# A graph layer with gathered rows: TensorE's waits for its own signals at reused PSUM slots

## The chip, the cores and the metric

The kernel runs on one core of one Trainium2 chip. The metric is the device time of that core in microseconds. The kernel before takes 18844.27 us, the median of three runs (18839.44 to 18869.69 us). One further execution was taken with the hardware profiler; it has its own, different time, given below.

## The reference

The layer works on a graph of 50,000 nodes with 160 features each and 1,650,000 directed edges, which come sorted by their destination. For each edge the features of the source node are multiplied with the four numbers of the edge (one scalar, one 3-vector) and with five small weight matrices; the messages are summed by destination node, multiplied with two more matrices, passed through a relu, added to the node's features twice, and normalised:

```python
s = x[:, :64];  v = x[:, 64:].reshape(n, 32, 3)
ss, vv = s[src], v[src]                      # gather by edge
e0, e1 = sh[:, 0:1], sh[:, 1:4]
out0 = C0 * (ss*e0 @ W1 + dot(vv, e1)*INV3 @ W2)
out1 = C1 * (p3(ss, W3, e1) + p4(vv*e0, W4) + p5(cross(vv, e1), W5))
m_agg = segment_sum(concat(out0, out1), dst)
h = concat(m_agg[:, :64] @ Ws * LIN_S, einsum(m_agg[:, 64:], Wv) * LIN_V)
x = layernorm(x + (x + relu(h)))
```

Everything after the gather is linear in the gathered row up to the relu, so a row of x can be summed per destination and per edge number first, and multiplied by combined weights afterwards.

## The kernel before, in words

**Tiling.** An edge slot is one of 128 partitions; 128 edges are a unit, six units a group, two groups a pair. There are 1,044 pairs. For each unit one indirect DMA on GpSimd's queue (POOL, L319 in `gather`) fetches 128 rows of x, one for each partition, into a sixth of a group's half of a tile `xg`; 12,522 such gathers make the whole edge list. The pool of `xg` holds four tiles, so four pairs can be in flight.

**Sums.** For each pair VectorE builds a selection matrix `ha` (L328, L331), 32 destinations by four edge numbers for each unit, and TensorE multiplies it with the gathered rows (L343 in `group_sums`), six matmuls adding up in each half of a PSUM tile `ps`. VectorE then turns the result into `sums` (L349). The pool `psA` has two slots for `ps`.

**Weights and nodes.** Four groups are a chunk of 128 sums. `apply_weights` multiplies a chunk by the weights (L579, five matmuls into the PSUM tile `phc`), and ScalarE copies it out. For each block of 128 nodes `own` makes the share of the node's own edge: two transposes of x into the PSUM tile `ptx` (L622), a copy by ScalarE to `xT` (L624), and twice two matmuls into a PSUM tile `yx` (L630), read by VectorE (L634, L636). `block` gathers the chunks that touch the block (L646, PSUM tile `phb`), adds, and starts the normalisation. The tiles `phc`, `ptx`, `yx` and `phb` share one tag, `misc`, in the pool `psM`, which has two slots.

**Order.** The program is written pair by pair; a table `later` (function `after_pair`) names what is to be issued after which pair: for a block, `do_ahead` (load x), four pairs later `do_own`, then `do_weights`, `do_block` and so on. A tile framework then draws the dependences between instructions and between a tile and the tile that had its slot before, orders each engine's instructions, and puts semaphore waits where a dependence needs one. An engine counts its finished work on a semaphore of its own; the one of TensorE is also waited for by TensorE itself, where it writes into a slot that it has written before: in the pair loop 1,280 of TensorE's matmuls carry such a wait (412 at L579, 337 at L646, 295 at L630, 234 at L343, 2 at L622).

Besides, the edge list is packed in the background: VectorE and SyncE rewrite the edges without the nodes' own edge into DRAM (`pack`), whose rows are loaded for later pairs.

Of the kernel before, what the change touches and what calls it, by code (L numbers as in the profile page):

```python
# [51 lines left out]
D = MUL0 + 3 * MUL1  # L52
# [10 lines left out]
W = 32  # L63
QG = P // W
FB = P // NK
ND = D // FB
# [38 lines left out]
def tile_gnn_resnorm(ctx: ExitStack, tc: tile.TileContext, x, src, dst, attr, W1, W2, W3, W4, W5, Ws, Wv, out, n_edges):  # L105
    nc = tc.nc
    N = x.shape[0]
    NBLK, NB, GA, G, NU, NG, L, NH, NR, FAR = plan(N, n_edges)
# [7 lines left out]
    ident = const.tile([P, P], F32, name="ident")  # L116
# [6 lines left out]
    BWh = const.tile([D // 2, 2, NK, D], F32, name="BWh")  # L123

    BWk = const.tile([P, ND, D], F32, name="BWk")
# [99 lines left out]
    with tc.tile_pool(name="once", bufs=1) as once, tc.tile_pool(name="raw", bufs=2) as rawp, \  # L225
# [98 lines left out]
        def spread(placed, u, n):  # L324
# [8 lines left out]
                                    .to_broadcast([P, n, NK, W]), op=ALU.mult)  # L333
            return ha

        def group_sums(p, rows, ha, at, i):


            s, g0, ng = pairs[p]
            ps = psA.tile([P, PG, D], F32, name="ps")  # L340
            rows, got = rows
            for j, xr in enumerate(rows):
                mm = nc.tensor.matmul(ps[:, j // G, :], ha[:, j].rearrange("p k w -> p (k w)"), xr,  # L343
                                      start=j % G == 0, stop=j % G == G - 1)

                if j == 0 and p + 1 < len(pairs):
                    for r in got[1:]:
                        tc.add_manual_dep(mm.ins, r.name, LANDED)
            nc.vector.transpose(at[:, :, i:i + ng, :].rearrange("p b g w -> p g b w"),  # L349
                                ps[:, :ng].rearrange("p g (b f) -> p g b f", f=FB))  # L350
# [224 lines left out]
        def apply_weights(at, ng):  # L575

            ph = psM.tile([P, D], F32, name="phc", tag="misc")
            for b in range(ND):
                nc.tensor.matmul(ph[:ng * W], at[:, b, :ng].rearrange("p g w -> p (g w)"), BWk[:, b, :], start=b == 0, stop=b == ND - 1)  # L579
            hp = hpp.tile([P, D], F32, name="hp")  # L580
            evict(hp[:ng * W], ph[:ng * W])  # L581
            return hp, ng * W

        def rows_of(b):
            nb = min(P, N - b * P)
            return nb, slice(b * P, b * P + nb)
# [6 lines left out]
        def ahead(bs):  # L593

            nb = rows_of(bs[0])[0]
            n0, n1 = rows_of(bs[0])[1].start, rows_of(bs[-1])[1].stop
            xt = aheadp.tile([P, BP, D], F32, name="xt")
            dq.dma_start(xt[:nb, :len(bs)], x[n0:n1, :].rearrange("(h n) d -> n h d", h=len(bs)))

            assert rows_stored[0] == NR or row_start(rows_stored[0])[1][0] >= n1  # L600
            sa = aheadp.tile([P, BP, NK], F32, name="sa")
            dq.dma_start(sa[:nb, :len(bs)],
                         selves[0, n0 * NK:n1 * NK].rearrange("(h n k) -> n h k", h=len(bs), k=NK))
            return [(xt[:, h], sa[:, h]) for h in range(len(bs))]
# [8 lines left out]
                                    rr[:, :len(cs)].unsqueeze(2).to_broadcast([P, len(cs), P]), op=ALU.is_equal)  # L613
            return hot2

        def own(b, xt, sa):

            nb, row = rows_of(b)
            H = D // 2
            pt = psM.tile([H, 2, P], F32, name="ptx", tag="misc")  # L620
            for i in range(2):
                nc.tensor.transpose(pt[:, i, :nb], xt[:nb, i * H:(i + 1) * H], ident[:nb, :nb])  # L622
            xT = np_.tile([H, 2, P], F32, name="xT")
            evict(xT[:, :, :nb], pt[:, :, :nb])  # L624
            t = aheadp.tile([P, D], F32, name="t")
            for h in range(NK // 2):
                y = psM.tile([P, 2, D], F32, name="yx", tag="misc")
                ks = slice(2 * h, 2 * h + 2)
                for i in range(2):
                    nc.tensor.matmul(y[:nb], xT[:, i, :nb], BWh[:, i, ks, :], start=i == 0, stop=i == 1)  # L630
                for i in range(2):
                    k = 2 * h + i
                    if k == 0:
                        nc.vector.tensor_scalar(t[:nb], y[:nb, i], sa[:nb, 0:1], None, op0=ALU.mult)  # L634
                    else:
                        nc.vector.scalar_tensor_tensor(t[:nb], y[:nb, i], sa[:nb, k:k + 1], t[:nb],  # L636
                                                       op0=ALU.mult, op1=ALU.add)
            return xt, t

        def block(b, xt, t, hot2):  # L640
            nb, row = rows_of(b)
            cs = of_block[b]
            ph = psM.tile([P, D], F32, name="phb", tag="misc")
            for i, c in enumerate(cs):
                hp, r = hps[c]
                nc.tensor.matmul(ph[:nb], hot2[:r, i, :nb], hp[:r], start=i == 0, stop=i == len(cs) - 1)  # L646
            nc.vector.tensor_tensor(ph[:nb], ph[:nb], t[:nb], op=ALU.add)  # L647
            return norm1(np_, ph[:nb], xt[:nb], nb)

# [5 lines left out]
        for h, (eng, period) in enumerate(HELP.items()):  # L655
            first = PG * G + h * period // 2
            nbatch = P // ROWS[eng]
            while True:
                at = [int(first + i * period / nbatch) // (PG * G) for i in range(nbatch)]
# [3 lines left out]
                s, g, ng = pairs[q]  # L663
# [47 lines left out]


        later = {}

        def after_pair(p, f, *args):
            later.setdefault(p, []).append((f, args))

        hps, of_nodes, resid, rstds, outs = {}, {}, {}, {}, {}
# [6 lines left out]
        def do_ahead(b):  # L725
            bs = together(b)
            if b == bs[0]:
                of_nodes.update(zip(bs, ahead(bs)))

        def do_own(b):  # L730
            of_nodes[b] = own(b, *of_nodes.pop(b))
# [30 lines left out]
        def examine_all():  # L762

            far = chunk_
            parts = [(c0, c1, near(c0 + 1) - near(c0), *bounds[c0]) for c0, c1 in zip(cuts, cuts[1:])]
            for c0, c1, each, low, high in parts:
                nc.vector.tensor_scalar(far[:, c0:c1], far[:, c0:c1], -each, c0 * each - near(c0) - (low + high) / 2,
                                        op0=ALU.mult, op1=ALU.add)
            nc.vector.tensor_tensor(far, far, rowid, op=ALU.add)
            for c0, c1, each, low, high in parts:  # L770
                nc.vector.tensor_scalar(far[:, c0:c1], far[:, c0:c1], 2 / (high - low), None, op0=ALU.mult)
            checks = ((extremes[:, 0], ALU.min, 0.0, ALU.is_lt), (extremes[:, 1], ALU.max, W - 1.0, ALU.is_gt),
                      (packed[:, 0], ALU.min, 0.0, ALU.is_lt), (packed[:, 1], ALU.max, 0.0, ALU.is_gt),
                      (counts[:, 0], ALU.min, 0.0, ALU.is_lt), (counts[:, 0], ALU.max, 0.0, ALU.is_gt),
                      (counts[:, 1], ALU.min, W / 2, ALU.is_lt),
                      (strayed, ALU.min, 0.0, ALU.is_lt), (strayed, ALU.max, 0.0, ALU.is_gt),
                      (far, ALU.min, -1.0, ALU.is_lt), (far, ALU.max, 1.0, ALU.is_gt))
            worst = once.tile([P, len(checks)], F32, name="worst")
            wrong = once.tile([P, len(checks)], F32, name="wrong")
            for i, (what, op, limit, cmp) in enumerate(checks):  # L780
                nc.vector.tensor_reduce(worst[:, i:i + 1], what, axis=AX.X, op=op)
                nc.vector.tensor_scalar(wrong[:, i:i + 1], worst[:, i:i + 1], float(limit), None, op0=cmp)
            bad = once.tile([P, 1], F32, name="bad")
            nc.vector.tensor_reduce(bad, wrong, axis=AX.X, op=ALU.max)
            pb = psM.tile([1, 1], F32, name="pb", tag="misc")
            nc.tensor.matmul(pb, bad, ones[:, 0:1], start=True, stop=True)
            nc.vector.tensor_scalar(more[:, 0:1], pb, 1.0, None, op0=ALU.min)
            nc.vector.tensor_scalar(more[:, 1:2], pb, 1.0, float(NB), op0=ALU.min, op1=ALU.mult)
# [4 lines left out]
        START = 2  # L793
        AHEAD = 7
        raws, has, flags = {}, {}, []
# [14 lines left out]
        for at, bs in zip(complete, after):  # L810
            for b in bs:
                after_pair(max(at - AHEAD, START - 1), do_ahead, b)
                after_pair(max(at - AHEAD + 4, START), do_own, b)
        later_pools.enter_context(tc.manual_schedule(engines={ET.SP}))
        for p, (s, g, ng) in enumerate(pairs):
# [68 lines left out]
    with tc.tile_pool(name="up", bufs=1) as up, tc.tile_pool(name="us", bufs=2) as us, tc.For_i(0, once_more, 1):  # L884
        nc.gpsimd.iota(base, pattern=[[NBLK, NB]], base=0, channel_multiplier=0, allow_small_or_imprecise_dtypes=True)
        dall = up.tile([P, JU, P], I32, name="dall")
        mm = up.tile([P, 2, JU], F32, name="mm")
# [14 lines left out]
        for s in range(nseg):  # L902
# [7 lines left out]
            for c in range(CB):  # L910
# [3 lines left out]
                at = us.tile([PB, 2, SEG], F32, name="at")  # L914
# [18 lines left out]
    with tc.tile_pool(name="edges2", bufs=2) as ep, tc.tile_pool(name="ops2", bufs=2) as op, \  # L933
            tc.tile_pool(name="node2", bufs=1) as np_, tc.tile_pool(name="psA2", bufs=2, space=PSUM) as psA, \
            tc.tile_pool(name="psF2", bufs=1, space=PSUM) as psF:
        with tc.For_i(0, blocks, 1) as b:
# [5 lines left out]
            with tc.For_i(u0, u1, GA) as u:  # L942
# [21 lines left out]
                ps = psA.tile([NBLK, 2, 512], F32, name="ps2")  # L964
                for j in range(GA):
                    for h in range(2):
                        nc.tensor.matmul(ps[:, h, 0:2 * D], hot[:, j, :], xa[:, j, 2 * h:2 * h + 2, :],
                                         start=j == 0, stop=j == GA - 1)
# [3 lines left out]
            for h in range(2):  # L972
                pt = psF.tile([D // 2, NK, P], F32, name="pt2")
                for k in range(NK):
                    nc.tensor.transpose(pt[:, k, :NBLK], acc[:, k, h * (D // 2):(h + 1) * (D // 2)], ident[:NBLK, :NBLK])
                at = np_.tile([D // 2, NK, NBLK], F32, name=f"ac{h}")
                nc.scalar.copy(at, pt[:, :, :NBLK])
                parts.append(at)
            ph = psF.tile([NBLK, D], F32, name="ph2")
# [45 lines left out]
```

## Time and profile before

| what | value |
|---|---|
| median of three runs | 18844.27 us |
| the profiled execution, its own time | 15704.38 us |
| span of its trace, first to last instruction | 15702.1 us |
| granted clock of TensorE | 0.724 |
| gathers on POOL, L319 | 12,522, 947 ns each |
| POOL busy | 11859.1 us (76%) |
| TensorE busy | 8274.5 us (53%) |
| VectorE busy | 6000.0 us (38%) |
| ScalarE busy | 498.2 us (3%) |
| DMA | mean 77 GB/s, q0 (the gathers) 24.6% of 16 engines' span |

The profiled execution is shorter than the runs without a profile by a factor of 15704.38 / 18844.27 = 0.833. Durations below are those of the profiled execution. A row of the profile names the line, the engine, what is written and read, how often, the total and mean time of one, and then how long the engine had been idle just before these instructions and what ended that idle time; "issue" is idle time that no signal in the trace explains.

### The profile page before, as it was taken

Reading aid. Unit: us, or ns where it says so; the run is one execution under the profiler, and the core shown is the slowest. Engines: PE = TensorE matmul, PEld = TensorE weight load, DVE = VectorE, ACT = ScalarE, POOL = GpSimd, SP = SyncE. Lnnn points to the kernel's source line nnn. Section 1 sums busy time; section 2 is a strip of 40 time slices with the busy share of each in tenths; the row PEclk is TensorE's granted clock in tenths of the full one; section 3 lists DMA queues with packets and bytes.
Section 4 is the critical chain, followed back from the end, with each engine's and each line's share of the span. In section 5 each row is a group of like instructions: output and inputs, shape, how many; then the busy total and the mean of one; then the engine's idle time right before and its main releaser. Section 6 shows DMA issues by size and latency. Waiting matters only on the chain. (4 is left out here: it accounts for less than half of the span.)

```text
span 15702.1 us, 120546 instructions
## 1 busy us (share of the span) xinstructions
PE 8274.5 (53%) x38505; PEld 7583.2 (48%) x38506; DVE 6000.0 (38%) x11070; ACT 498.2 (3%) x1392; POOL 11859.1 (76%) x12536
## 2 busy tenths in 40 slices
PE   4554555545555555555555555555555555555455
PEld 4444445445454444444444444444444445444454
DVE  5343433424334343443433434243343433434332
ACT  0000000000000000000000000000000000000000
POOL 7777777777777777777777777777777777777777
PEclk7777777777777776777777777777777767777677
DMA  2322222232322222222232232322223232222222
GB/s 79 86 73 84 74 77 80 72 86 73 85 73 77 81 73 78 80 76 81 73 86 72 77 82 72 86 72 78 79 74 85 72 86 73 75 80 73 75 74 67
DMA packets 797530, 1215.80 MB, mean 77 GB/s; under 512 B 271491, under 2 KB 575800, under 8 KB 792918
## 3 DMA queue, kind: packets, MB, share of 16 engines
q0 software_dynamic: 601056, 1026.60, 24.6%
q1 hardware_dynamic: 194410, 180.15, 3.9%
q8 instruction: 323, 5.29, 0.1%
q14 instruction: 301, 2.47, 0.1%
q10 hardware_dynamic: 1440, 1.29, 0.0%
HBM read 1135.77 MB, written 71.40 MB: 77 GB/s over the span
## 5 line engine op out<-in xcount | busy, mean ns | idle before, releaser
L319 POOL DMA_INDIRECT xg<-in_x,si x12522 | 11854.8, 947 | 3824.4 <-issue 3784.1
L343 PE MATMUL ps<-xg,ha 128*128 128x160 f32 x25044 | 5770.9, 411 | 7141.4 <-DMA xg<-in_x,si 5348.5
L343 PEld LDWEIGHTS ps<-xg,ha 128*128 128x128 f32 x25044 | 5512.6, 283 | 7455.4 <-issue 6701.9
L349 DVE STREAM_TRANSPOSE sums<-ps 128x320 f32<-128x320 f32 x1044 | 536.6, 515 | 7498.8 <-PE ps L343 7472.8
L331 DVE TENSOR_TENSOR ha<-hot,pk 128x1536 f32<-128x1536 f32 x1044 | 1805.9, 1731 | 64.4 <-PE ps L343 64.4
L630 PE MATMUL yx<-BWh,xT 80*128 80x320 f32 x3128 | 1099.9, 498 | 125.3 <-ACT xT L624 123.0
L579 PE MATMUL phc<-BWk,sums 128*128 128x160 f32 x5220 | 852.6, 312 | 11.6 <-DVE t L636 10.2
L630 PEld LDWEIGHTS yx<-BWh,xT 80*128 80x128 f32 x3128 | 642.1, 216 | 423.7 <-ACT xT L624 195.4
L579 PEld LDWEIGHTS phc<-BWk,sums 128*128 128x128 f32 x5220 | 788.7, 201 | 23.8 <-issue 20.1
L634 DVE TENSOR_SCALAR t<-yx,sa 128x160 f32<-128x160 f32 x391 | 147.0, 376 | 1414.3 <-PE yx L630 1412.2
L328 DVE TENSOR_TENSOR hot<-bank,rel 128x384 f32<-128x384 f32 x1044 | 557.5, 540 | 0.1
L646 PE MATMUL phb<-hp,hot 128*128 128x160 f32 x3474 | 550.7, 303 | 0.8 <-ACT hp L581 0.8
L646 PEld LDWEIGHTS phb<-hp,hot 128*128 128x128 f32 x3474 | 499.7, 192 | 24.7 <-issue 23.1
L636 DVE SCALAR_TENSOR_TENSOR t<-yx,sa,t 128x160 f32<-128x160 f32 x1173 | 438.4, 374 | 67.6 <-PE yx L630 59.7
L511 DVE COPY_PREDICATED prow<-marks,prow 128x2370 f32<-128x2370 int32 (+8 forms) x160 | 443.0, 2769 | 0.0
L581 ACT COPY hp<-phc 128x160 f32<-128x160 f32 x522 | 151.0, 289 | 7862.4 <-PE phc L579 7819.6
L624 ACT COPY xT<-ptx 80x256 f32<-80x256 f32 x391 | 143.5, 367 | 5866.1 <-PE ptx L622 5839.6
L511 DVE COPY_PREDICATED pra<-marks,pra 128x1580 f32<-128x1580 int32 (+8 forms) x160 | 303.6, 1898 | 0.0
L612 DVE TENSOR_TENSOR hot<-bank,rr 128x512 f32<-128x512 f32 (+2 forms) x391 | 285.1, 729 | 0.0
L647 DVE TENSOR_TENSOR phb<-phb,t 128x160 f32<-128x160 f32 x391 | 126.6, 324 | 109.1 <-PE phb L646 107.7
L622 PE MATMUL ptx<-ident,xt 128*80 128x128 f32 (+1 forms) x782 | 155.6, 279 | 20.6 <-ACT hp L581 18.4
L194 ACT ACTIVATE rstd<-mv,eps_t 128x1 f32<-128x1 f32 x391 | 115.2, 295 | 1334.1 <-DVE mv L189 1329.6
(144 smaller groups left out, 2612.5 us busy)
## 6 DMA issues: line engine op xcount, KB each, us to landing
xg<-in_x,si POOLq DMA_INDIRECT x12522
edges<-prow SPq DMA_DIRECT2D x1994, 18.5 KB
r<-edges SPq DMA_DIRECT2D x99, 360.0 KB
selves<-mine SPq DMA_DIRECT2D x1992, 0.5 KB
xt<-in_x SPq DMA_DIRECT2D x195, 160.0 KB
out<-o SPq DMA_DIRECT2D x195, 160.0 KB
pra<-in_attr SPq DMA_DIRECT2D x15, 1580.0 KB
pri<-in_src SPq DMA_DIRECT2D x15, 395.0 KB
```

The costliest lines, as they stand in the source:

```text
L319: got.append(nc.gpsimd.indirect_dma_start(out=xg[:, j, :], out_offset=None, in_=x, in_offset=bass.IndirectOffsetOnAxis(ap=placed[0][:, u + ...
L328: nc.vector.tensor_tensor(hot[:, :n], slotsP[:, 0:W].unsqueeze(1).to_broadcast([P, n, W]), rel[:, u:u + n].unsqueeze(2).to_broadcast([P, n ...
L331: nc.vector.tensor_tensor(ha[:, :n], hot[:, :n].unsqueeze(2).to_broadcast([P, n, NK, W]), pk[:, :, u:u + n].rearrange("p k u -> p u k").un ...
L343: mm = nc.tensor.matmul(ps[:, j // G, :], ha[:, j].rearrange("p k w -> p (k w)"), xr, start=j % G == 0, stop=j % G == G - 1)
L349: nc.vector.transpose(at[:, :, i:i + ng, :].rearrange("p b g w -> p g b w"), ps[:, :ng].rearrange("p g (b f) -> p g b f", f=FB))
L511: nc.vector.copy_predicated(what[:n, a:e], mi[:, r].unsqueeze(2).to_broadcast([n, e - a, what.shape[2]]), what[:n, a + d:e + d])
L579: nc.tensor.matmul(ph[:ng * W], at[:, b, :ng].rearrange("p g w -> p (g w)"), BWk[:, b, :], start=b == 0, stop=b == ND - 1)
L612: nc.vector.tensor_tensor(hot2[:, :len(cs)], slotsP.unsqueeze(1).to_broadcast([P, len(cs), P]), rr[:, :len(cs)].unsqueeze(2).to_broadcast( ...
L622: nc.tensor.transpose(pt[:, i, :nb], xt[:nb, i * H:(i + 1) * H], ident[:nb, :nb])
L630: nc.tensor.matmul(y[:nb], xT[:, i, :nb], BWh[:, i, ks, :], start=i == 0, stop=i == 1)
L636: nc.vector.scalar_tensor_tensor(t[:nb], y[:nb, i], sa[:nb, k:k + 1], t[:nb], op0=ALU.mult, op1=ALU.add)
L646: nc.tensor.matmul(ph[:nb], hot2[:r, i, :nb], hp[:r], start=i == 0, stop=i == len(cs) - 1)
```

## The change

A list `written` records, for each of the two kinds of PSUM slot (`ps` and `misc`), the matmuls that have written each tile. `wrote` declares to the framework, for a matmul that writes a tile, that it has no dependence on the matmuls of the tile allocated two before, which is the one that had the same slot. It is called for the first matmul of each half of `ps`, and for every matmul of `phc`, `ptx`, `yx` and `phb`. Nothing is declared about the readers on VectorE and ScalarE.

Besides, `own` is cut in two: `turned` has the two transposes and the copy to `xT`, `own` the four matmuls and what follows. `do_turned` is entered in the table just ahead of `do_own`, after the same pair.

```diff
+        written = {"misc": [], "ps": []}
+        def fresh(kind):
+            written[kind].append([])
+        def wrote(kind, ins):
+            ws = written[kind]
+            for old in ws[-3] if len(ws) > 2 else []:
+                tc.declare_no_dep(ins.ins, old, reason="its reader has waited for it")
+            ws[-1].append(ins.ins)
+            return ins
...
             ps = psA.tile([P, PG, D], F32, name="ps")
+            fresh("ps")
...
+                if j % G == 0:
+                    wrote("ps", mm)
+                else:
+                    written["ps"][-1].append(mm.ins)
...
             ph = psM.tile([P, D], F32, name="phc", tag="misc")
+            fresh("misc")
             for b in range(ND):
-                nc.tensor.matmul(ph[:ng * W], ...)
+                wrote("misc", nc.tensor.matmul(ph[:ng * W], ...))
...
-        def own(b, xt, sa):
+        def turned(b, xt, sa):
             pt = psM.tile([H, 2, P], F32, name="ptx", tag="misc")
+            fresh("misc")
             for i in range(2):
-                nc.tensor.transpose(pt[:, i, :nb], ...)
+                wrote("misc", nc.tensor.transpose(pt[:, i, :nb], ...))
             xT = np_.tile([H, 2, P], F32, name="xT")
             evict(xT[:, :, :nb], pt[:, :, :nb])
+            return xt, sa, xT
+        def own(b, xt, sa, xT):
...
+        def do_turned(b):
+            of_nodes[b] = turned(b, *of_nodes.pop(b))
...
+                after_pair(max(at - AHEAD + 4, START), do_turned, b)
                 after_pair(max(at - AHEAD + 4, START), do_own, b)
```

The matmuls of `yx` and `phb` are wrapped in the same way as those of `phc`.

More of the change, by code (lines that the diff above doesn't have):

```diff
@@ L577, in apply_weights @@
             ph = psM.tile([P, D], F32, name="phc", tag="misc")
+            fresh("misc")
             for b in range(ND):
-                nc.tensor.matmul(ph[:ng * W], at[:, b, :ng].rearrange("p g w -> p (g w)"), BWk[:, b, :], start=b == 0, stop=b == ND - 1)
+                wrote("misc", nc.tensor.matmul(ph[:ng * W], at[:, b, :ng].rearrange("p g w -> p (g w)"), BWk[:, b, :],
+                                               start=b == 0, stop=b == ND - 1))
             hp = hpp.tile([P, D], F32, name="hp")
@@ L614, in nodes @@
             return hot2
-        def own(b, xt, sa):
+        H = D // 2
+        def turned(b, xt, sa):
             nb, row = rows_of(b)
-            H = D // 2
             pt = psM.tile([H, 2, P], F32, name="ptx", tag="misc")
+            fresh("misc")
             for i in range(2):
-                nc.tensor.transpose(pt[:, i, :nb], xt[:nb, i * H:(i + 1) * H], ident[:nb, :nb])
+                wrote("misc", nc.tensor.transpose(pt[:, i, :nb], xt[:nb, i * H:(i + 1) * H], ident[:nb, :nb]))
             xT = np_.tile([H, 2, P], F32, name="xT")
             evict(xT[:, :, :nb], pt[:, :, :nb])
+            return xt, sa, xT
+        def own(b, xt, sa, xT):
+            nb, row = rows_of(b)
             t = aheadp.tile([P, D], F32, name="t")
@@ L627, in own @@
                 y = psM.tile([P, 2, D], F32, name="yx", tag="misc")
+                fresh("misc")
                 ks = slice(2 * h, 2 * h + 2)
                 for i in range(2):
-                    nc.tensor.matmul(y[:nb], xT[:, i, :nb], BWh[:, i, ks, :], start=i == 0, stop=i == 1)
+                    wrote("misc", nc.tensor.matmul(y[:nb], xT[:, i, :nb], BWh[:, i, ks, :], start=i == 0, stop=i == 1))
                 for i in range(2):
@@ L643, in block @@
             ph = psM.tile([P, D], F32, name="phb", tag="misc")
+            fresh("misc")
             for i, c in enumerate(cs):
                 hp, r = hps[c]
-                nc.tensor.matmul(ph[:nb], hot2[:r, i, :nb], hp[:r], start=i == 0, stop=i == len(cs) - 1)
+                wrote("misc", nc.tensor.matmul(ph[:nb], hot2[:r, i, :nb], hp[:r], start=i == 0, stop=i == len(cs) - 1))
             nc.vector.tensor_tensor(ph[:nb], ph[:nb], t[:nb], op=ALU.add)
@@ L785, in examine_all @@
             pb = psM.tile([1, 1], F32, name="pb", tag="misc")
+            fresh("misc")
             nc.tensor.matmul(pb, bad, ones[:, 0:1], start=True, stop=True)
```

## The prediction

> **What bounds the kernel now.** I read the page's first part, then the costliest groups, then who waits for whom on TensorE, then the timeline of a stretch in the middle, then the chain that ended last. The first part shows no engine full:
>
> ```profile
> span 15702.1 us, 120546 instructions
> PE 8274.5 (53%) x38505; PEld 7583.2 (48%) x38506; DVE 6000.0 (38%) x11070; ACT 498.2 (3%) x1392; POOL 11859.1 (76%) x12536
> ```
>
> POOL at 76% looks as if it had a quarter to spare. The groups say otherwise (after the bar: busy time, mean ns of one, then the idle time just before and what ended it):
>
> ```profile
> L319 POOL DMA_INDIRECT xg<-in_x,si x12522 | 11854.8, 947 | 3824.4 <-issue 3784.1
> L343 PE MATMUL ps<-xg,ha 128*128 128x160 f32 x25044 | 5770.9, 411 | 7141.4 <-DMA xg<-in_x,si 5348.5
> ```
>
> POOL's idle time is a step between gathers, not a wait: 3784.1 of 3824.4 us has no releaser. Busy and idle together are (11854.8 + 3824.4) / 12522 = 1.2521 us for each gather. TensorE's idle time (7141.4 us ahead of L343) ends mostly when gathered rows land. The timeline of POOL shows the step:
>
> ```profile
> 8004.84 0.94 POOL L319 DMA_INDIRECT xg<-in_x,si  x1 [0.30 <-issue]
> 8006.09 0.95 POOL L319 DMA_INDIRECT xg<-in_x,si  x1 [0.30 <-issue]
> 8007.34 0.95 POOL L319 DMA_INDIRECT xg<-in_x,si  x1 [0.30 <-issue]
> 8008.59 0.95 POOL L319 DMA_INDIRECT xg<-in_x,si  x1 [0.30 <-issue]
> ```
>
> and that of TensorE in the same stretch a pair's matmuls which begin after 8.42 us of waiting for rows:
>
> ```profile
> 8007.47 6.46 PE L343 MATMUL ps<-xg,ha 128*128 128x160 f32 x24 [8.42 <-DMA xg<-in_x,si]
> ```
>
> So the span is: first gather at 9.5 us, last at 15683.2 us, 12,521 steps of (15683.2 - 9.5) / 12521 = 1.2518 us between them, and 18.9 us of tail: 9.5 + 15673.7 + 18.9 = 15702.1. A pace set by TensorE would show as POOL steps of unequal length. Going through the starts of all gathers in the trace, only 13 steps are longer than 1.5 times the median of 1.251 us; together they are 18.3 us too long. POOL sets the end, from start to tail.
>
> **The waits in question, in the profile.** TensorE's waits, the longest and those at the lines that the change names:
>
> ```profile
> PE ps L343 <- DMA xg<-in_x,si: 5348.5, 699, 18.6
> PE ps L343 <- issue: 1405.6, 215, 12.7
> PE yx L630 <- ACT xT L624: 123.0, 239, 0.6
> PE phc L579 <- DVE t L636: 10.2, 6, 2.6
> PE phb L646 <- ACT hp L581: 0.8, 2, 0.4
> ```
>
> In this whole list no row has TensorE waiting for TensorE. And the 337 matmuls of `phb` that wait for TensorE's own signal have a second wait beside it, put in an instruction of its own on the weight-load queue:
>
> ```profile
> L646 PEldq EVENT_SEMAPHORE  x337: 51/51/51, 182.1 to 15650.3; - x169
> ```
>
> Shortest, median and longest are all 51 ns: a wait that is already fulfilled costs 51 ns of TensorE's queue, no more.
>
> [...] in the built program the awaited matmul stands a median of 20 to 34 instructions back (4 at L630). [...] no such wait ever shows. [...] the first matmul follows the start of its pair's last gather by 7.3 us (median over the pairs). [...]
>
> **The change part by part.**
>
> *The declarations.* They should take the 1,280 waits away. In the built program they take none: before and after, TensorE has the same 1,280 waits in the pair loop at the same matmuls, and all 59,856 instructions of all engines stand in the same order with the same operands, waits, values and signals; only source lines differ. My reading of why: the declarations remove dependences drawn between two instructions that touch one tile, while a new tile in an old slot is held back by the old tile's release, drawn later. Cost and gain on the chip: 0.
>
> *`own` cut in two.* `do_turned` and `do_own` are entered after the same pair, one behind the other, so the 782 transposes, 391 copies and 1,564 matmuls stay where they were. SP's and POOL's queues have the same DMAs in the same places. Cost: 0.
>
> Sum against the profiled execution: 15702.1 us of span and 2.3 us around it, 15704.4 us, unchanged. The runs without a profile take 18844.27 / 15704.38 = 1.1999 times as long. [...] At 1.2 times the step is 1.2518 x 1.2 = 1.502 us (an estimate), and POOL still bounds: TensorE would have 8274.5 x 1.2 = 9929 us of work in 18844. So I predict the same median, 18845 us.
>
> **If the waits did go.** The gain is bounded from both sides. Below: 1,280 x 0.051 = 65 us of TensorE's queue, a price from the row above; even if each cost what L630 waits for ScalarE, 123.0 / 239 = 0.51 us, it would be 659 us. Above that only the 1405.6 us of "issue" ahead of L343 could hide such waits, and those stretches of 6.5 us can't be a wait for matmuls dozens of places back, on an engine that had been idle since. Any of it lies in TensorE's idle 15702.1 - 8274.5 = 7428 us; what is late next is still the row that POOL has not yet asked for. On the path are only the last pair's `phc` and `phb`, behind the last gather:
>
> ```profile
> 15683.15 4.57 DMA xg<-in_x,si
> 15687.77 0.55 PE ps L343 x2
> 15688.75 1.60 PE phc L579 x10
> 15690.35 1.10 PE phb L646 x8
> ```
>
> A few waits of 51 ns: 0.2 us, or 0.001%. If the cover were gone (POOL faster than TensorE), the 65 us would be worth 65 / 15702 = 0.4%.
>
> **Rivals.**
>
> *The waits do go on the chip, and TensorE's start matters (0.02, faster).* Then POOL's 0.30 us ahead of each gather would hold waits for tiles that TensorE frees, and up to the whole 65 to 659 us could come off: 18844 - 1.2 x 65 = 18766 us down to 18053 us. Against it: the tile is freed once in 12 gathers, while the 0.30 us stands ahead of every one.
>
> *The declarations hold, but change nothing that counts (within the forecast).* 18844 us less 0.2 us: not to be told from the forecast by time, only by the program.
>
> *The cut in `own` delays TensorE until gathers wait (0.02, slower).* The place is the first gather into an `xg` tile, which has to wait for the matmuls of four pairs before. Over all pairs these ended a median of 37.4 us ahead of that gather, at least 14.6 us. A delay decides from there on: if the two transposes and the copy (0.38 and 0.37 us in the timeline) came to stand behind a late signal by 40 us in each of 391 blocks, 391 x (40 - 37.4) x 1.2 = 1220 us, 20064 us. Against it: the order is the same, and TensorE is idle 47% of the span, so it catches up between blocks.
>
> *The clock state differs from that of the runs before (0.03, faster).* [...] It says nothing of the change; I count it as faster, since the runs before already are at the slow ratio.
>
> *Plain scatter between runs.* The three runs before lie 30 us apart, 0.16%; a median of equal programs could by chance differ by over 0.2%: 0.01 on each side.
>
> **How the numbers follow.** The forecast, an unchanged program, has 0.91. 0.2%, or 38 us, is about what a measurement of this kernel can tell from no change. Faster: 0.02 + 0.03 + 0.01 = 0.06. Slower: 0.02 + 0.01 = 0.03. Same: 0.91. The range follows from the scatter of an equal program, the three runs' extremes widened by about half their distance on each side: 18815 to 18885 us; the rivals lie outside of it and together have less than 2 in 10.
>
> **What would show it.** In the profile after: again 12,522 gathers of 947 ns with about 3784 us of "issue"; 337 waiting instructions of 51 ns at the line of `phb`; TensorE busy within a few us of 8274.5; the same order in the timeline. If the number of those waiting instructions falls, the first step is wrong; if POOL's idle time gets a releaser on TensorE, the bound is misread. The time is wrong if the runs are at another clock, or if the step of POOL depends on something that this trace doesn't show[...].

## The result, and the profile after

| | before | changed |
|---|---|---|
| median of 12 runs each, side by side | 18862.19 us | 18856.39 us |
| lowest to highest | 18814.18 to 18902.09 us | 18827.03 to 18905.40 us |
| ratio, 95% interval | | 1.0002 [0.9991, 1.0012] |

No change, as forecast. But the profiled execution of the changed kernel is not the one that the prediction worked with. It took 18847.58 us, like the timed runs, where the profiled execution of before took 15704.38 us. One plain fact is needed to read what follows: the kernel before takes about 15710 us on some chips and about 18900 us on others (each chip was used once, so the chip and the moment are not told apart), and the profile of before shows the first kind, the profile after the second.

The page after, first part:

```profile
span 18845.2 us, 120546 instructions
PE 8598.3 (46%) x38505; PEld 7358.8 (39%) x38506; DVE 6004.6 (32%) x11070; ACT 501.9 (3%) x1392; POOL 11857.9 (63%) x12536
```

Every count is that of before. VectorE and POOL are busy for as long as before; TensorE for 4% longer. The groups (after the bar: busy time, mean ns, idle time just before and what ended most of it), with the lines renumbered by the change (L343 is now L359):

```profile
L319 POOL DMA_INDIRECT xg<-in_x,si x12522 | 11853.6, 947 | 6945.2 <-issue 3637.2
L359 PE MATMUL ps<-xg,ha 128*128 128x160 f32 x25044 | 5184.8, 366 | 3677.3 <-issue 2523.8
L660 PE MATMUL yx<-BWh,xT 80*128 80x320 f32 x3128 | 1512.7, 647 | 2841.2 <-ACT xT L648 1976.6
```

A gather still takes 947 ns. POOL's idle time is 6945.2 us instead of 3824.4 us, and those 3121 us are the difference between the two spans (18845.2 - 15702.1 = 3143 us) but for 22 us. Who ends it, from the list of POOL's waits (total us, times, longest):

```profile
POOL xg L319 <- issue: 3637.2, 11925, 1.6
POOL xg L319 <- remote: 1830.4, 465, 8.1
POOL xg L319 <- PE ps L359: 1194.8, 74, 43.4
POOL xg L319 <- PE ptx L646: 201.2, 12, 45.1
```

The first row is the fixed step of 0.30 us. "remote" is a signal for which the trace shows no instruction that ended then; the last two rows are TensorE's. Going through the starts of all gathers, the median step is 1.251 us, as in the profile before; 569 steps are longer than 1.5 times that, by 3151 us in all. Of 546 that are longer than 2.4 us, 540 stand ahead of the first gather of a pair, the one that needs a tile of the ring back from TensorE. So on this chip gathers do wait for TensorE. TensorE, in turn, hardly waits for rows any more (before, the same row had 5348.5 us, 699 times):

```profile
PE ps L359 <- DMA xg<-in_x,si: 186.6, 35, 20.5
```

Its first matmul of a pair starts a median of 33.0 us after the pair's last gather, where the profile before has 2.9 us: here the rows are early and TensorE is late.

Two simple causes can be set aside from the two pages. The packets of the gathers' queue take as long in both (24.6% of 15702.1 us and 20.4% of 18845.2 us, 3.86 and 3.84 ms for each of the 16 engines on average), so slower transfers of the rows are not it. The granted clock of TensorE is lower (0.663 against 0.724), but TensorE's busy time grows by 324 us only, a tenth of the 3143 us.

TensorE itself often stands still. Here is one such place, in its timeline and then ScalarE's:

```profile
5316.60 3.03 PE L359 MATMUL ps<-xg,ha 128*128 128x160 f32 x17
5319.46 0.38 PE L646 MATMUL ptx<-ident,xt 128*80 128x128 f32 x2
5366.13 4.10 PE L660 MATMUL yx<-BWh,xT 80*128 80x320 f32 x7 [46.29 <-ACT xT L648]
```

```profile
5365.71 0.37 ACT L648 COPY xT<-ptx 80x256 f32<-80x256 f32 x1 [130.23 <-remote]
```

The two transposes end, by the profile's model, at 5319.84 us. ScalarE, idle for 130 us, copies their result at 5365.71 us: by the model the signal of TensorE came 46 us late. (Since these ends are modelled, the trace doesn't tell a late signal from transposes that really ended late; below, both are called a late signal.) It is not the only one: of the 391 copies to `xT`, 145 start more than 5 us after the modelled end of their transposes, 7 in the profile before. POOL, whose ring was full by then, resumes 0.14 us after ScalarE:

```profile
5356.87 0.95 POOL L319 DMA_INDIRECT xg<-in_x,si  x1 [0.30 <-issue]
5365.85 0.94 POOL L319 DMA_INDIRECT xg<-in_x,si  x1 [8.04 <-remote]
```

None of this is the change's: the timed runs of the kernel before are as slow (18862.19 us), though no profile of that kernel on a slow chip exists. And the waits that the change names look the same as before:

```profile
L677 PEldq EVENT_SEMAPHORE  x337: 51/51/51, 221.0 to 18815.7; - x169
```

### The profile page after: what moved, and what is told of

Read it like the earlier page. It is cut to its first block, busy times and chain, and to the rows that moved or that the text cites. A ratio compares the mean times of both kernels' runs of the same rounds, so it can differ in the third digit from the quotient of the medians.

```text
span 18845.2 us, 120546 instructions
## 1 busy us (share of the span) xinstructions
PE 8598.3 (46%) x38505; PEld 7358.8 (39%) x38506; DVE 6004.6 (32%) x11070; ACT 501.9 (3%) x1392; POOL 11857.9 (63%) x12536
## 3 DMA queue, kind: packets, MB, share of 16 engines
q0 software_dynamic: 601056, 1026.60, 20.4%
## 4 chain that ended last, share of the span: by engine, by line
another core or an unknown queue 50%; issue 14%; POOL 13%; PE 13%; DVE 10%; ACT 1%; DMA 0%; DVEq 0%; ACTq 0%; POOLq 0%; SPq 0%
POOL xg L319 13%; PE ps L359 6%; PE yx L660 3%; DVE ha L331 2%; PE phc L600 2%; PE phb L677 1%; DVE prow L531 1%; DVE sums L369 1%; DVE hot L328 1%; DVE t L666 1%; DVE hot L634 0%; DMA xg<-in_x,si 0%; DVE pra L531 0%; PE ptx L646 0%
## 5 line engine op out<-in xcount | busy, mean ns | idle before, releaser
L319 POOL DMA_INDIRECT xg<-in_x,si x12522 | 11853.6, 947 | 6945.2 <-issue 3637.2
L359 PE MATMUL ps<-xg,ha 128*128 128x160 f32 x25044 | 5184.8, 366 | 3677.3 <-issue 2523.8
L359 PEld LDWEIGHTS ps<-xg,ha 128*128 128x128 f32 x25044 | 4782.6, 245 | 4172.0 <-issue 3088.2
L660 PE MATMUL yx<-BWh,xT 80*128 80x320 f32 x3128 | 1512.7, 647 | 2841.2 <-ACT xT L648 1976.6
L660 PEld LDWEIGHTS yx<-BWh,xT 80*128 80x128 f32 x3128 | 825.4, 278 | 3302.3 <-ACT xT L648 2080.0
L600 PE MATMUL phc<-BWk,sums 128*128 128x160 f32 x5220 | 1157.9, 359 | 1278.1 <-issue 798.5
L600 PEld LDWEIGHTS phc<-BWk,sums 128*128 128x128 f32 x5220 | 981.5, 235 | 1384.2 <-issue 982.0
L677 PE MATMUL phb<-hp,hot 128*128 128x160 f32 x3474 | 709.2, 344 | 560.9 <-issue 332.5
L677 PEld LDWEIGHTS phb<-hp,hot 128*128 128x128 f32 x3474 | 613.8, 224 | 610.3 <-issue 437.3
L646 PEld LDWEIGHTS ptx<-ident,xt 128*80 128x80 f32 (+1 forms) x782 | 95.1, 138 | 1108.7 <-ACT hp L603 675.2
L297 PE MATMUL bank<-ident,r 120*128 120x120 f32 x100 | 44.3, 443 | 550.9 <-DVE baseB L287 426.9
```

The source lines that it names most:

```text
L319: got.append(nc.gpsimd.indirect_dma_start(out=xg[:, j, :], out_offset=None, in_=x, in_offset=bass.IndirectOffsetOnAxis(ap=placed[0][:, u + ...
L600: wrote("misc", nc.tensor.matmul(ph[:ng * W], at[:, b, :ng].rearrange("p g w -> p (g w)"), BWk[:, b, :], start=b == 0, stop=b == ND - 1))
L646: wrote("misc", nc.tensor.transpose(pt[:, i, :nb], xt[:nb, i * H:(i + 1) * H], ident[:nb, :nb]))
L660: wrote("misc", nc.tensor.matmul(y[:nb], xT[:, i, :nb], BWh[:, i, ks, :], start=i == 0, stop=i == 1))
L677: wrote("misc", nc.tensor.matmul(ph[:nb], hot2[:r, i, :nb], hp[:r], start=i == 0, stop=i == len(cs) - 1))
```

## The experiments

Theory A is the prediction's: POOL's step sets the end. Theory B was formed from the profile after: where the span is 18845 us TensorE, with late signals, sets the pace. Three things were to be told apart: whether the waits are worth anything if they really go, what TensorE's pace counts for, and what bounds the two kinds of execution.

**The kernel before, unchanged.**

> The kernel before, unchanged, for a profile of it on the chip that times it. Theory A (the prediction's: POOL's step between gathers sets the end, at whatever clock): 18.85 ms with all 12,522 gathers one step apart[...]; no idle time of POOL ended by TensorE. Theory B (in the timed runs TensorE's signals come late and the gathers wait for tiles that it frees): 18.85 ms with a median step of 1.25 us, gathers of 947 ns, and about 3150 us of longer steps, as in the profile of the changed kernel.

Measured: 15706.13 us (15705.19 to 15707.81, 10 runs), ratio to the kernel before 1.000 [0.999, 1.0009]. The 18.85 ms that both theories expected did not come: this chip is of the quick kind, as it is for the next three experiments, so theory B could not show. The profile is like that of the prediction:

```profile
L319 POOL DMA_INDIRECT xg<-in_x,si x12522 | 11856.9, 947 | 3824.4 <-issue 3780.2
```

The step is 1.251 us in this execution and in that of 18845 us. The prediction's estimate of a step of 1.50 us where the time is 18.8 ms is refuted: POOL's work (947 ns a gather) and step are equal in both.

**The waits really gone.** PSUM tiles are allocated once and used in turn; nothing is left to wait for a tile's release, and TensorE's waits for its own signals fall from 1,280 to 103 (all at L314, the transposes into `pk`).

```diff
+        sumsP = [psA.tile([P, PG, D], F32, name=f"ps{i}") for i in range(2)]
+        miscP = [psM.tile([P, 2 * D], F32, name=f"misc{i}") for i in range(2)]
...
-            ps = psA.tile([P, PG, D], F32, name="ps")
+            ps = next_sums()
...
-            ph = psM.tile([P, D], F32, name="phc", tag="misc")
+            ph = next_misc(P, D)
```

(`ptx`, `yx`, `phb` and the tiles of the weights likewise.)

> The waits really go: PSUM tiles allocated once and used in turn, instead of a new tile for each use, so TensorE keeps only 103 of its 1,280 waits for its own signals (and those for older work); what each engine computes is as before, the order differs in about 5% of TensorE's places. Theory A: 18850 us, within 0.2%, since the waits cost 51 ns each beside other work. Theory B with the waits on the path: faster by 65 us (51 ns each) up to 700 us. Theory B with the waits not the cause: within 0.3%.

Measured: 15706.13 us, ratio 1.000 [0.9991, 1.0009]. As theory A has it, though not at the 18850 us of the expectation: where POOL sets the end, 1,177 waits less are worth nothing that can be measured.

**Less work for TensorE and VectorE.**

```diff
-            for h in range(NK // 2):
+            for h in range(1):
                 y = psM.tile([P, 2, D], F32, name="yx", tag="misc")
```

> Leaves out half of each node's own share: the second pair of matmuls into yx and their two additions on VectorE, 782 matmuls and 782 additions less; the result lacks that part. Theory A: 18850 us within 0.2%, since POOL has the same 12,522 gathers. Theory B: TensorE has 4% less to do, so 18850 us falls by 1 to 4%, to 18100 to 18660 us.

Measured: 15706.39 us, ratio 0.9999 [0.9991, 1.0008]. TensorE's busy time falls from 8265.0 (the kernel before on this chip) to 7822.2 us and the time doesn't move: on this chip TensorE is not on the path. The same kernel was measured on a second chip, which was quick too:

> The kernel that leaves out half of each node's own share once more, for a chip where the kernel before takes 18850 to 18950 us. Theory B (there TensorE, slowed while gathers run, sets the pace): 1 to 4% faster, ratio 0.96 to 0.99. Theory A (POOL alone): ratio 1.000 within 0.002. Where the kernel before takes 15706 us: 15706 us, as before.

Measured: 15734.91 us beside 15736.37 us, ratio 0.9999 [0.999, 1.0008]. So the direct test of theory B, less work for TensorE on a slow chip, is missing.

**A deeper ring of gathered rows.**

```diff
-            tc.tile_pool(name="rows", bufs=4) as rowp, \
+            tc.tile_pool(name="rows", bufs=5) as rowp, \
-            tc.tile_pool(name="far", bufs=3) as farp, \
+            tc.tile_pool(name="far", bufs=2) as farp, \
...
-            hot = op.tile([P, PG * G, W], F32, name="hot")
+            hot = farp.tile([P, PG * G, W], F32, name="hot")
```

(`farp` is otherwise unused here.)

> Five instead of four tiles in the ring of gathered rows (the selection tiles hot take two instead of three to make room). Theory A: 18850 us within 0.2%. Theory B: a gather waits one pair (15 us) later for TensorE, so the 3150 us of long steps fall by a tenth to a half: 17300 to 18500 us.

Measured: 15705.82 us, ratio 1.000 [0.9991, 1.0008], as theory A has it on a quick chip.

**One gather in twelve left out.** This and the next two experiments are on a chip of the slow kind (the kernel before: 18859.59 us).

```diff
-            for j in range(n - len(others)):
+            for j in range(n - n // 12):
...
-            return [xg[:, j, :] for j in range(n - len(others))] + others, got
+            return [xg[:, min(j, n - n // 12 - 1), :] for j in range(n)], got
```

> Leaves out one gather in twelve: the last unit of a pair is multiplied with the rows of the unit before it, so those sums are not the reference's. Everything else is issued as before. Theory A (POOL's step sets the end): 1,043 gathers less at 1.2518 us are 1306 us, so 15706 falls to 14400 us (on a chip where the kernel before takes 18850 us: theory A with a longer step gives 17280 us, theory B, late signals of TensorE, gives 18300 us or more).

Measured: 17459.3 us (two runs), ratio 0.9257 [0.9239, 0.9276], 1400 us less. Both numbers missed: theory A with a longer step had 17280 us, theory B 18300 us or more. Removing 1,043 gathers takes away their 1.251 us each (1305 us) and 95 us besides:

```profile
L319 POOL DMA_INDIRECT xg<-in_x,si x11479 | 10866.8, 947 | 6541.7 <-issue 3312.2
```

The steps that are too long still add up to 3059 us (3151 us with all gathers). So on a slow chip the time is very nearly the gathers at POOL's step plus some 3.1 ms of waits at the ring. TensorE had the same work and got it done in 1400 us less, with fewer gathers; theory B's fixed pace of TensorE is too simple.

**No gathers at all, with and without the waits.** Only the first pair's rows are gathered, and all pairs use them.

```diff
-            tc.tile_pool(name="rows", bufs=4) as rowp, \
+            tc.tile_pool(name="rows", bufs=1) as rowp, \
...
+            if kept:
+                return [kept[0][:, j, :] for j in range(n)], []
             xg = rowp.tile([P, PG * G, D], F32, name="xg")
+            kept.append(xg)
```

> Takes POOL's cover away: only the first pair's rows are gathered, and all pairs use them, so the sums are not the reference's; TensorE, VectorE, ScalarE and SyncE do what they did. The 1,280 waits of TensorE for its own signals stay. Theory A: POOL no longer sets the end; TensorE (8274 us busy) or VectorE (6000 us) with what they wait for each other does: 8000 to 10000 us. Theory B says nothing else.

> As the kernel without gathers, with PSUM tiles allocated once, so that the waits of TensorE for its own signals are gone but for 103. It measures what the waits are worth with the cover gone. The prediction's price: 1,177 x 51 ns = 60 us less than the kernel without gathers, if TensorE is then the bound (0.6 to 0.8%); at the upper price of 0.51 us 600 us less; none, if VectorE is the bound. The order of a few per cent of the instructions differs too, and reads of PSUM by ScalarE and VectorE get waits for each other, so 1% either way can come from that.

Measured, on the same slow chip: 6913.24 us (6909.06 to 6915.88) with the waits, 6901.20 us (6895.93 to 6905.42) without; ratios to the kernel before 0.3666 [0.366, 0.3672] and 0.3658 [0.3652, 0.3664]. The first parts of the two pages:

```profile
span 6906.9 us, 102427 instructions
PE 6103.6 (88%) x38505; PEld 5603.1 (81%) x38506; DVE 5924.6 (86%) x11070; ACT 504.0 (7%) x1392; POOL 15.9 (0%) x26
```

```profile
span 6903.4 us, 101966 instructions
PE 6121.5 (89%) x38505; PEld 5608.9 (81%) x38506; DVE 5924.9 (86%) x11070; ACT 503.8 (7%) x1392; POOL 15.8 (0%) x26
```

With the cover gone the second kernel is 12 us faster, which would be 10 ns for each of 1,177 waits, not 51. But this isn't the price of the waits alone: in the trace VectorE has 541 more waits for ScalarE, and ScalarE 534 more for VectorE, than with the waits, and the 12 us are the sum of both. TensorE is busy for 88% and VectorE for 86%, so part of what TensorE saves may also be lost in waiting for VectorE (not shown). The forecast of 8000 to 10000 us was too high too: in the run without gathers TensorE's granted clock is 0.947, and its busy time 6103.6 us, where the profile before, from which the forecast took its 8274 us, has a granted clock of 0.724.

More important: on this chip, without gathers, TensorE does all its work in 6.9 ms and waits at most 1.3 us for the copies to `xT`, where the longest such wait was 46.3 us in the profile after:

```profile
PE yx L635 <- ACT xT L629: 128.5, 245, 1.3
PE yx L660 <- ACT xT L648: 1976.6, 188, 46.3
```

Only 5 of the 391 copies start more than 5 us after their transposes. With eleven of twelve gathers, on this same chip, the longest such wait is 40.7 us. A slow TensorE is not a property of the chip alone; it comes with the gathers.

**The waits gone, on the slow chip.**

> The same kernel with the waits gone, for the case that this call is run on a chip where the kernel before takes 18850 us. There: theory B with the waits on the path, faster by 65 to 700 us; theory B with the waits not the cause, within 0.3%. On a chip where the kernel before takes 15706 us: 15706 us within 0.1%, as before.

Measured: 18836.66 us (20 runs) beside 18859.59 us, ratio 0.9986 [0.998, 0.9993]: 23 us by the medians (0.12%), below the 65 us of the lower price. Here too the order of TensorE's work and the waits between ScalarE and VectorE differ, so that the 23 us aren't shown to be the waits'. Its POOL row is the slow one, with all of the 3.1 ms:

```profile
L332 POOL DMA_INDIRECT xg<-in_x,si x12522 | 11854.6, 947 | 6915.1 <-issue 3645.1
```

So the waits are not what costs those 3.1 ms.

**Five, six and three tiles in the ring.** For the long waits of POOL a theory C was set against B: that TensorE's signals are held back while gathers run without a pause. The kernel with five tiles is the one above. Six tiles (three tiles in the same way, with `bufs=3` and no other edit; the kernel of six has fewer tiles in other pools as well):

```diff
-            tc.tile_pool(name="rows", bufs=4) as rowp, \
+            tc.tile_pool(name="rows", bufs=6) as rowp, \
...
```

> Five tiles in the ring of gathered rows, for a chip where the kernel before takes 18850 us. Theory B (TensorE with its late signals has a throughput limit of 18 us a pair): 18850 us within 1%, whatever the ring. Theory C (TensorE's signals are withheld while gathers follow each other without a pause, and come through some 4 us after the ring has made POOL pause; with four tiles 546 pauses, about one in (4 - 2) = 2 pairs): one pause in three pairs, 348 of 5.8 us, 2.0 ms in place of 3.15 ms: 17700 us. Where the kernel before takes 15706 us: 15706 us.

> Six tiles in the ring; to make room, hot and ha have two tiles instead of three, the output two instead of three, hp one less. Theory B: 18850 us within 1%, or slower through the smaller pools. Theory C: one pause in four pairs, 261 of 5.8 us, 1.5 ms: 17200 us. Where the kernel before takes 15706 us: 15706 us, up to 1% more if two tiles of ha make TensorE late enough.

> Three tiles in the ring. Theory B: 18850 us to 19500 us. Theory C: a pause in every pair, 1,044 of 5.8 us, 6.0 ms: 21700 us. Where the kernel before takes 15706 us: the least slack of 14.6 us goes to nothing in a few pairs: 15710 to 15850 us.

Measured, on another slow chip (the kernel before: 18946.14 us): five tiles 18773.68 us (three runs), ratio 0.9907 [0.9887, 0.9926]; six tiles 19242.14 us (three runs), 1.0152 [1.0133, 1.0172]; three tiles 18926.59 us, 0.9992 [0.9984, 0.9999]. Theory C's 17700, 17200 and 21700 us are all wrong, in both directions. The pauses longer than 2.4 us number 568, 523 and 578, where theory C had 348, 261 and 1,044. How far gathers may run ahead hardly counts. That what comes through TensorE per unit of time counts instead is theory B's side; it fits, with the reservation of the eleven gathers, but is not shown. With five and six tiles POOL is held up at another place as well (844.3 us with five), so these two don't test the ring alone; three tiles show no such wait. Of six tiles' waits,

```profile
POOL xg L319 <- DVE si L303: 1526.7, 103, 40.6
```

that is the list of indices for the next twenty groups, which is itself made behind TensorE. Six tiles also had smaller pools elsewhere, so their 1.5% have no single cause.

Five tiles beat the kernel before by 0.9% on this slow chip and equal it on the quick one. Of the kernels that compute the whole result, that is the largest gain that the runs found.

## Why the prediction was right, and where its reasons were not

**The declarations take no waits away: right.** The change measures 1.0002, the kernel against itself 1.000, and the 337 waiting instructions at `phb` are there again at 51 ns. The traces of before and after both have 1,280 of TensorE's instructions in the pair loop with a wait for its own signals, at the same matmuls (412, 337, 295, 234 and 2). The reason given, that the waits come from a tile's release, is supported by the kernel in which the tiles are never released: there they are gone. It was not shown inside the framework.

**`own` cut in two costs nothing: right.** It is in the same ratio.

**The number itself, 18845 us, had luck in it.** That an equal program gives an equal time was reasoned well: the ratio is 1.000 for the kernel before against itself on a quick chip, and 1.0002 for the change on a slow one. That the time came out at 18.86 ms needed a slow chip again: the kernel before takes 15706 us on a quick one.

**POOL's step sets the end: right for the execution it was read from, wrong for the runs it was applied to.** On quick chips less work for TensorE, no waits or a deeper ring all leave 15706 us, and the step carries the whole span. On slow chips the step is the same and 3151 us of waits at the ring are added. The prediction named the sign in advance: if POOL's idle time gets a releaser on TensorE, the bound is misread. It did, with 1194.8 us at L359.

**"At 1.2 times the step is 1.2518 x 1.2 = 1.502 us": this is the step of the reasoning that failed.** It takes the ratio of the two times, 1.1999, for one factor by which all of POOL's and TensorE's work is slower. That was the author's estimate; no trace or run had shown it. The measurement decides against it: a gather takes 947 ns and its step 1.251 us in the execution of 18847.58 us, where 1.136 and 1.502 us would be needed. Two facts ought to have warned: the ratio of two single times doesn't tell where the time goes, and the forecast didn't need the estimate, since it rests on the two programs being equal, whatever the bound.

**TensorE "within a few us of 8274.5": wrong,** 8598.3 us. The number came from a quick chip and was compared with a slow one; the change didn't cause the difference.

**Two smaller slips.** The first matmul of a pair follows the start of the pair's last gather by a median of 2.9 us in the profile before, not 7.3 us; about 5% of the pairs are above 7.3 us. The rows still land after POOL's work: in the prediction's chain the last gather's DMA takes 4.57 us, beside 0.95 us for a gather on POOL. And the lower end of the range, 18815 us, lies 24 us below the lowest of the three runs, not half of their distance (15 us).

**The price of a wait, 51 ns, and the gain of 0.4% with the cover gone: too high, as far as it was measured.** 12 us of 6913 us, 0.17%, or 10 ns a wait, with the other waits that came in. The rival in which the waits do go and TensorE's start matters had 65 to 659 us (times 1.2); on a slow chip, where gathers do wait for TensorE, the kernel without the waits gains 23 us. That is under a third of the lower end even if all of it is the waits', and under the 0.2% that count as a change.

## What to carry to other kernels

Before a declaration about waits is priced, look in the built program whether a wait went; dependences of reused tiles may come from another place than the one declared, and allocating the tiles once did remove them. The waits that show their shortest duration everywhere (51/51/51) were worth less than that here: nothing where POOL sets the pace, and in net 10 and 20 ns each in the other two kernels without them (12 and 23 us for 1,177). Where the profiled execution and the timed runs differ as here (15704.38 and 18844.27 us), the profile need not show what bounds the timed runs: get one of the timed kind before naming a bound, and don't take the ratio for one factor on all work.

## What the runs showed of the hardware

The same program has two speeds: medians of 15707 and 15736 us on two chips, and of 18860 and 18946 us on two others, and on each chip all runs of it lie within 0.5% of each other. Since each of these chips was used once, it stays open whether the chip itself makes the difference or something that went on at the time. POOL's, VectorE's and ScalarE's instructions take the same time in both, within 0.5% in these: a gather 947 and 947 ns, VectorE's step from `ps` to `sums` 515 and 513 ns, ScalarE's copy to `xT` 367 and 367 ns. At 18845 us TensorE's instructions come, for stretches of some 12 us, one at a time at multiples of 0.70 us, although the trace shows no wait that holds them: of the steps between its records (matmuls, weight loads and the small instructions of its queues), 2,046 lie between 0.65 and 0.75 us and 1,613 between 1.35 and 1.45 us, where the quick profile has 88 and 49. From the timeline of TensorE after:

```profile
9616.64 0.42 PE L600 MATMUL phc<-BWk,sums 128*128 128x160 f32 x1 [2.25 <-issue]
9618.75 0.43 PE L600 MATMUL phc<-BWk,sums 128*128 128x160 f32 x1 [1.69 <-issue]
9621.54 0.42 PE L600 MATMUL phc<-BWk,sums 128*128 128x160 f32 x1 [2.36 <-issue]
```

These are consecutive matmuls of one group without any wait between them. SyncE's issue of a store, 0.23 us in the quick profile, takes 0.69 us in the same stretch, and three of these issues (9617.32, 9620.11 and 9622.90 us) start 0.03 to 0.04 us ahead of a weight load of TensorE (9617.35, 9620.15 and 9622.94 us). So in this stretch the two queues go in step, while POOL keeps its step of 1.25 us; what ties them, no run shows. Besides there are the late signals, up to 46 us. Both go with the gathers: on a chip where the kernel with gathers is slow, the one without has 70 and 7 such steps, 5 late copies instead of 145, and TensorE at 88%. TensorE is not limited by its own rate of instructions either: that kernel sustains 38,505 matmuls in 6906.9 us, 5.6 in each us at a granted clock of 0.947, and the profile after has 2.0 at 0.663 (38,505 in 18845.2 us). What the gathers do to TensorE on such a chip, whether POOL's own work or the transfers do it, and why other chips are free of it, stays open; whether less work for TensorE helps there wasn't measured.
